# Column sums of six ctx blocks formed by accumulating transfers and two products, in a fused cross-attention and LoRA feed-forward kernel

## The chip, the cores and the metric

The kernel runs on one core of a Trainium2 chip. The metric is device time in microseconds (us) of one execution; several executions are taken and their median is given. The kernel before took 1082.93 us (median of three, 1082.42 to 1084.54). One further execution was recorded by the hardware profiler.

The core has five engines, each with an instruction queue that is worked off in order: PE (TensorE, matrix products, with its weight loads listed as PEld), DVE (VectorE), ACT (ScalarE), POOL (GpSimd) and SP (SyncE, used here to issue transfers). Sixteen DMA engines move data; transfers can be issued from the queues of SP, ACT and POOL. An engine that waits for another one's result, or for a transfer to land, waits at a semaphore, and everything behind that instruction in its queue waits too.

## What is computed

Two batches `b` of 1024 rows and 2048 columns go through two layers. The first is a product of two fake-quantised matrices, the second a linear layer with low-rank additions. Cut to what matters here:

```
q(v, s, z) = (clip(round(v / s + z), 0, 255) - z) * s
x = x + q(layernorm(x)) @ q(ctx)          # ctx: 2048 x 2048 for each b
x = x + ffn(layernorm(x))                 # kernel 2048 x 2048, bias, LoRA A and B by gate, shared LoRA
```

The kernel keeps the quantised values as whole numbers centred on 128, that is from -128 to 127, which 16-bit floats hold exactly. With c1 the centred x and c2 the centred ctx, and d1 = 128 - z1, d2 = 128 - z2, the product of one row and one column is

```
s1*s2 * ( sum_k c1*c2  +  d2 * rowsum(c1)  +  d1 * colsum(c2)  +  D*d1*d2 )
```

The column sums `colsum(c2)` are what the change is about: for each batch b and each block n of 512 columns of ctx, 512 sums over 2048 rows, wanted on all 128 partitions.

## The kernel before

**Tiling.** ctx comes in eight blocks (b, n), n = 0 to 3. A block of 2048 x 512 values is brought in as eight slices r of 128 partitions x 2 x 512 values (`lit` tiles, 512 KB each, loaded by SP). For every slice, ACT scales, rounds and clips below (`round_ctx`, L458, into one of three `q2b` tiles), and DVE clips above, subtracts 128 and writes bf16 into the block's two `big` tiles (`centre_ctx`, L464). A block's products with c1 (`Pair.products`, L530) go to PSUM for each of four groups g of 256 rows of x, each in two halves j. ACT or DVE add the column term and the row term to PSUM (`Pair.begin`, L526, before the products; `Pair.late`, L543, after them), and DVE scales and adds to `y` (`Pair.end`, L547).

**Column sums before the change.** `column_term` calls four steps. `column_parts` (L486) runs 16 products on PE, one for each 128 rows of the block, each with 32 columns of ones, so that four of them fill four strips of one PSUM tile `pcp`. `column_copy` (L499, DVE) brings the tile to SBUF. `column_mean` (L505, PE, float32, two passes) multiplies it with a matrix of 1/32, which adds the four strips and spreads the sum over all partitions (`pc`). `column_end` (L511, DVE) forms `d1 * colsum + D*d1*d2` in a `bp` tile, which `begin` and `late` read.

**Order.** For batch 0 the text STEPS sets the order of the entry: DVE, ACT and PE follow it step by step, each in its own part (`in_order`). In it V16 to V23 centre block (0,2), `u2 p2 c2 v2` are the four steps of its column term, `M2.0.0.6.7` and `M2.0.1.0.7` are products of that block, and `L2.0.0 L2.0.1` add its column term afterwards. Outside the entry a scheduler, with a cost model of its own, sets the order on each engine when the kernel is built. Block (0,3) is quantised during the products of block (0,2). Blocks (1,0) and (1,1) are quantised in the last outer step (o = 6) of the feed-forward of batch 0, from `meanwhile`; blocks (1,2) and (1,3) during the products of batch 1.

**Feed-forward.** Seven outer times seven inner products (Strassen's scheme, twice) in float32: `product` (L828), `spread` (L852), combinations of operands on POOL for the left side (`lit`, L762 and L771) and on DVE for the right side (`big`). `Delta.step` adds the low-rank part; its first two `bp` tiles of a batch come by a transfer that POOL issues (L679), the others by ACT.

Of the kernel before, what the change touches and what calls it, by code (L numbers as in the profile page):

```python
# [9 lines left out]

F32 = mybir.dt.float32
BF16 = mybir.dt.bfloat16
U8 = mybir.dt.uint8
I16 = mybir.dt.int16
AF = mybir.ActivationFunctionType
ALU = mybir.AluOpType
# [4 lines left out]
P = 128  # L21
# [4 lines left out]
QMAX = 255.0  # L26
CENTRE = 128.0
# [52 lines left out]
EARLY = [(0, 0), (1, 0), (2, 0)]  # L80
ROWS_ON_SCALAR = ()
PLACED_BY_SCALAR = (2, 3, 4, 5, 6, 7)


class Bufs:
# [13 lines left out]
def tile_quant_xattn_then_lora_ffn(  # L99
# [17 lines left out]
    nc = tc.nc  # L117
# [28 lines left out]
    lit = Bufs([const.tile([P, KQ, GT], F32, tag=f"lit{i}", name=f"lit{i}") for i in range(10)])  # L146
    q2b = Bufs([const.tile([P, 2, NB], I16, tag=f"q2b{i}", name=f"q2b{i}") for i in range(3)])

    acat = const.tile([P, KT, GPB // 2 * 3, R], F32, tag="acat", name="acat")
    own_col = [0, 2, 3, 5]  # L150

# [2 lines left out]
    axT = const.tile([P, GPB // 2, GT], F32, tag="axT", name="axT")  # L154
    gmat = const.tile([P, 2, GPB // 2, RC], F32, tag="gmat", name="gmat")
    st1 = const.tile([P, MT, NN, 6], F32, tag="st1", name="st1")
    st2 = const.tile([P, MT, NN, 6], F32, tag="st2", name="st2")
    r_s = const.tile([P, MT], F32, tag="r_s", name="r_s")

    zs = [  # L160
# [6 lines left out]

    def bf(t, n):

        return t.rearrange("p k n -> p (k n)").bitcast(BF16).rearrange("p (k n) -> p k n", n=n)  # L170

    def flat(t):
        return t.rearrange("p k n -> p (k n)")
# [91 lines left out]
    load_x(0, 3)  # L265
    ahead[0] = 10
    load_next()
    gate_b = const.tile([P, GB, NL], F32, tag="gate_b", name="gate_b")
    nc.sync.dma_start(
        out=gate_b.rearrange("p b n -> p (b n)"), in_=gate.rearrange("b n -> (b n)").partition_broadcast(P)  # L270
    )
# [23 lines left out]

    ident = const.tile([P, P], F32, tag="ident", name="ident")
    make_identity(nc, ident)
    ident_h = const.tile([P, P], BF16, tag="ident_h", name="ident_h")
    nc.gpsimd.tensor_copy(ident_h, ident)
    ones_h = const.tile([P, P], BF16, tag="ones_h", name="ones_h")  # L300
    nc.gpsimd.memset(ones_h, 1.0)


    zeros_h = const.tile([P, P], BF16, tag="zeros_h", name="zeros_h")
    nc.gpsimd.memset(zeros_h, 0.0)
    mean_w = const.tile([P, P], F32, tag="mean_w", name="mean_w")
    nc.gpsimd.memset(mean_w, 1.0 / 32)

# [8 lines left out]

    def gate_values():

        m_ad = const.tile([P, NL], F32, tag="m_ad", name="m_ad")  # L320
# [45 lines left out]
    class XTile:  # L366


        def __init__(self, b, m, c1T, wk):
            self.b, self.m, self.nm = b, m, f"{b}_{m}"  # L370
            self.on_vector = b == 0 and m not in ROWS_ON_SCALAR
            g, tok = m // MG, ds((m % MG) * P, P)
            self.y = y[g][:, m % MG, :]

            wf = flat(wk)
            self.q8 = wf[:, ds((m % 2) * (D // 4), D // 4)].bitcast(U8)
            self.qh = wf[:, D // 2 : D].bitcast(BF16)
            self.to = [c1T[g][:, ds(h * KH, KH), tok] for h in range(2)]
            self.pt = [None, None]

# [37 lines left out]
            )  # L418

        def turn(self, h):  # L420
            self.pt[h] = ps_m.tile([P, KH, P], BF16, tag="pm", name=f"pt_{self.nm}_{h}")
            for kt in range(KH):
                nc.tensor.transpose(self.pt[h][:, kt, :], self.qh[:, ds(h * H + kt * P, P)], ident_h)

# [23 lines left out]
            x.place(h)  # L448
        x.total()

    def quantise(c2, r):

        centre_ctx(c2, r, round_ctx())

    def round_ctx():
        buf, t = next_loaded(1)
# [3 lines left out]
        load_next()  # L460
        return qi

    def centre_ctx(c2, r, qi):
        nc.vector.tensor_scalar(c2[r // 4][:, ds(2 * (r % 4), 2), :], qi, QMAX, CENTRE, ALU.min, ALU.subtract)  # L464
        q2b.give(qi)

    def take_c2():
        bufs = [big.take() for _ in range(2)]
        return bufs, [bf(t, NB) for t in bufs]

    colt = {}
    pairs = []

    def column_term(b, n, c2):

        of = column_parts(b, n, c2)
        column_copy(of)
        column_mean(b, n, of)
        column_end(n, of)

    def column_parts(b, n, c2):

        parts = ps_m.tile([P, NB], F32, tag="pm", name=f"pcp_{b}_{n}")
        for k in range(KT):
            row = P // 4 * (k % 4)
            nc.tensor.matmul(  # L486
                parts[row : row + P // 4, :],
                ones_h[:, 0 : P // 4],
                c2[k // 8][:, k % 8, :],
                start=(k < 4),  # L490
                stop=(k >= KT - 4),
                skip_group_check=True,
            )
        return [parts]
# [18 lines left out]
    class Pair:  # L513
# [35 lines left out]
        def stats(self):  # L549
            for j in range(MG):  # L550
                nc.vector.bn_stats(  # L551
                    st2[:, self.g * MG + j, self.n, :], y[self.g][:, j, ds(self.n * NB, NB)]
                )

    def xattn_pair(b, n, g, c1T, c2):
# [66 lines left out]
    def prep_z(b, m, zq, wk):  # L622

        nm = f"{b}_{m}"
        g, tok = m // MG, ds((m % MG) * P, P)
        mean, rstd = norm_stats(st2[:, m], f"z{nm}")
# [295 lines left out]
    def entry():  # L922

        X = [XTile(0, m, c1T, wk) for m in range(MT)]
        qi, parts, at, ad = {}, {}, {}, {}
        idle = ps_acc.tile([P, MG, NB], F32, tag="delta", name="idle")
        recent = [(idle, 0)]
        tick = const.tile([P, 1], BF16, tag="tick", name="tick")

        def pair(n, g):  # L930
            if (n, g) not in at:
# [1 line left out]
            return at[n, g]  # L933

        def products(n, g, j, first, last=None):
            recent.append((pair(n, g).pa, j))
# [19 lines left out]
        def centred(r):  # L956
            if r // NR not in c2:
                next_block(0)
            centre_ctx(c2[r // NR], r % NR, qi.pop(r))

        def sums(n):
            parts[n] = column_parts(0, n, c2[n])

        def keep_busy(n):

            to, j = recent[-1]
            for i in range(n):
                nc.tensor.matmul(
                    to[:, j, :],
                    zeros_h,  # L970
                    (tick if to is idle else ones_h[:, 0:1]).to_broadcast([P, NB]),
                    start=(to is idle),
                    stop=True,
                    skip_group_check=True,
                )

        run = {
            "S": lambda m, n: X[m].stats(n),
# [9 lines left out]
            "Q": rounded,  # L988
            "V": centred,
            "u": sums,  # L990
            "p": lambda n: column_copy(parts[n]),
            "c": lambda n: column_mean(0, n, parts[n]),
            "v": lambda n: column_end(n, parts[n]),
            "B": lambda n, g, j: pair(n, g).begin(j),
            "M": products,
# [6 lines left out]
            "h": ad_copy,  # L1002
            "i": ad_turn,
            "j": lambda n: lora_a_place(n, ad[n]),
            "z": keep_busy,
# [14 lines left out]
    for b in range(B):  # L1020
# [9 lines left out]
        else:  # L1030
# [5 lines left out]
            for g in range(2, GPB):  # L1036
                for m in range(g * MG, (g + 1) * MG):
                    with tc.issue_after(opened.ins):
                        prep_x(b, m, c1T, wk)
                for n in range(2):  # L1040
                    xattn_pair(b, n, g, c1T, c2[n])
                    if g + 1 == GPB:
                        next_block(n)
                        if n == 0:
                            for r in range(NR):
                                quantise(c2[2], r)
# [9 lines left out]
        for g in range(GPB):  # L1056
            if (b, g) != (0, 0):
                xattn_pair(b, 2, g, c1T, c2[2])
            for r in {0: range(3), 1: range(3, 6), 2: range(6, 8), 3: ()}[g]:
                quantise(c2[3], r)  # L1060
            if 1 <= g <= 2:
                lora_a_step(b, g + 1)
            if g == 2:
# [53 lines left out]
        def meanwhile(o, s):  # L1117
# [23 lines left out]
                load_x(nb, m, slice(half * H, (half + 1) * H))  # L1141
            if s < 4:
                for r in range(2 * s, 2 * s + 2):
                    quantise(c2[0], r)
            if 1 <= s <= 4:
                prep_x(nb, s - 1, state["c1T"], state["wk"])
            if s == 3:
# [2 lines left out]
                c2[1] = [bf(c2b[1][0], NB)]  # L1150
            if s == 4:
                for r in range(2):
                    quantise(c2[1], r)
                c2b[1].append(big.take())
                c2[1].append(bf(c2b[1][1], NB))
            if s == 5:
                for r in range(2, 5):
                    quantise(c2[1], r)
            if s == len(INNER) - 1:
                for r in range(5, NR):  # L1160
                    quantise(c2[1], r)
# [62 lines left out]
```

## Time and profile before

| | |
|---|---|
| median of three executions | 1082.93 us (1082.42 to 1084.54) |
| the profiled execution | 1082.56 us |
| its span, from the first to the last instruction | 1080.8 us |
| PE busy | 1054.6 us (98%) |
| DVE busy | 766.6 us (71%) |
| ACT busy | 247.4 us (23%) |
| POOL busy | 253.8 us (23%) |
| transfers issued by POOL | 4 (`bp<-bd`, 256 KB each) |
| granted TensorE clock | 1.0 |

Numbers such as 84.80 are microseconds from the start of the span. A row of a group gives how often an instruction ran and its duration; for matrix products that duration includes their pipeline, so that the time between the starts of two of them, not the duration, is what one costs PE in a row. "To landing" is the time from the issue of a transfer to the semaphore that tells of its end.

### The profile page before, as it was taken

The page shows a single profiled execution, that of the slowest core. Times are in us where ns is not written, and L with a number is a line of the kernel's source. Part 1 is how long each engine was busy: PE and PEld are TensorE (multiplying, and loading weights), DVE is VectorE, ACT ScalarE, POOL GpSimd, SP SyncE. Part 2 cuts the span into 40 slices and gives each one's busy share as a digit, 9 for nine tenths or more (in the row PEclk, how much of TensorE's full clock was granted, in tenths as well). Part 3 has the DMA queues.
Part 4 walks back from the last instruction along what each step waited for, and adds up shares of the span by engine and source line. Part 5 has one row for each costly group of instructions (what it writes and reads, how often), then busy time and mean ns, then how long its engine had stood idle before and what let it go on. Part 6 is the DMA issues. An engine that isn't in the chain of part 4 may idle for free.

```text
span 1080.8 us, 10609 instructions
## 1 busy us (share of the span) xinstructions
PE 1054.6 (98%) x3932; PEld 489.8 (45%) x3932; DVE 766.6 (71%) x949; ACT 247.4 (23%) x351; POOL 253.8 (23%) x104
## 2 busy tenths in 40 slices
PE   5999999999999999999999999999999999999998
PEld 2443345544444444444444444554444444444443
DVE  7986867578877676677859655674969667756851
ACT  5866133210000000001675741331000000000000
POOL 0000003032435302533000000032244531253600
PEclk9999999999999999999999999999999999999999
DMA  9979645788798476699673292559889874748611
GB/s 341 381 196 308 190 176 190 256 316 295 263 339 324 160 264 217 191 372 321 230 246 119 98 266 103 198 210 360 294 269 297 288 269 148 264 146 301 214 39 58
DMA packets 119228, 257.15 MB, mean 238 GB/s; under 512 B 11272, under 2 KB 15496, under 8 KB 118152
## 3 DMA queue, kind: packets, MB, share of 16 engines
q1 hardware_dynamic: 98688, 215.05, 58.4%
q10 hardware_dynamic: 20168, 40.38, 10.7%
q0 software_dynamic: 320, 1.05, 0.4%
q8 instruction: 31, 0.51, 0.2%
q14 instruction: 21, 0.17, 0.1%
HBM read 220.79 MB, written 37.75 MB: 239 GB/s over the span
## 4 chain that ended last, share of the span: by engine, by line
PE 83%; DVE 8%; DMA 4%; ACT 3%; issue 1%; SPq 0%; ACTq 0%
PE fu L828 34%; PE fv L828 17%; PE pa L530 12%; PE fw L828 9%; PE pl L694 3%; PE px L648 3%; PE ptz L632 2%; DMA lit<-in_ctx_dram 2%; DVE st L551 2%; DVE st L383 1%; ACT q2b L458 1%; DVE y L547 1%; ACT big L412 1%; DVE big L771 1%; PE pg_b L574 1%
## 5 line engine op out<-in xcount | busy, mean ns | idle before, releaser
L828 PE MATMUL fu<-big,lit 128*128 128x512 f32 x896 | 395.3, 593 | 0.0
L828 PEld LDWEIGHTS fu<-big,lit 128*128 128x128 f32 x896 | 168.6, 190 | 206.3 <-issue 204.9
L530 PE MATMUL pa<-big,big 128*128 128x512 bf16 x1024 | 237.1, 381 | 7.3 <-ACT pa L526 3.4
L771 POOL TENSOR_TENSOR lit<-lit,lit 128x1024 f32<-128x1024 f32 x56 | 164.7, 2950 | 189.7 <-PE fw L828 74.6
L828 PE MATMUL fv<-big,lit 128*128 128x512 f32 x448 | 197.9, 594 | 0.0
L771 DVE TENSOR_TENSOR big<-big,big 128x2048 f32<-128x2048 f32 x56 | 164.4, 2935 | 0.7
L530 PEld LDWEIGHTS <-big 128*128 128x128 bf16 x1024 | 97.1, 98 | 136.3 <-issue 29.6
L762 POOL TENSOR_TENSOR lit<-lit,lit 128x1024 f32<-128x1024 f32 x32 | 85.7, 2677 | 256.4 <-DMA lit<-zs 230.4
L852 DVE TENSOR_TENSOR y<-y,fu 128x1024 f32<-128x1024 f32 x92 | 108.5, 1215 | 40.6 <-PE fu L828 40.2
L828 PEld LDWEIGHTS fv<-big,lit 128*128 128x128 f32 x448 | 84.3, 190 | 105.0 <-issue 104.7
L458 ACT ACTIVATE q2b<-lit,sc,inv 128x1024 int16<-128x1024 f32 x64 | 76.4, 1232 | 163.7 <-DMA lit<-in_ctx_dram 147.1
L852 DVE TENSOR_TENSOR y<-y,fv 128x1024 f32<-128x1024 f32 x48 | 56.8, 1218 | 78.8 <-PE fv L828 78.8
L762 DVE TENSOR_TENSOR big<-big,big 128x2048 f32<-128x2048 f32 x40 | 101.8, 2546 | 0.0
L828 PE MATMUL fw<-big,lit 128*128 128x512 f32 x224 | 99.4, 592 | 0.0
L683 ACT COPY pl<-bias 128x1024 f32<-128x1024 f32 x16 | 16.3, 1018 | 294.1 <-DVE y L705 258.1
L679 POOL DMA_DIRECT2D bp<-bd x4 | 2.6, 660 | 344.3 <-DMA bd<-q2b 166.3
L852 DVE TENSOR_TENSOR y<-y,fw 128x1024 f32<-128x1024 f32 x24 | 28.4, 1218 | 53.9 <-PE fw L828 53.9
L828 PEld LDWEIGHTS fw<-big,lit 128*128 128x128 f32 x224 | 42.1, 190 | 50.7 <-issue 50.7
L547 DVE SCALAR_TENSOR_TENSOR y<-pa,k_s,y 128x1024 f32<-128x1024 f32 x32 | 41.0, 1280 | 32.2 <-PE pa L530 32.1
L526 ACT ACTIVATE pa<-bp,r_s 128x512 f32<-128x512 f32 x58 | 39.0, 685 | 87.0 <-PE pa L530 57.1
L705 DVE TENSOR_TENSOR y<-pl,y 128x512 f32<-128x512 f32 x64 | 39.8, 679 | 17.5 <-PE pl L694 17.2
L383 DVE BATCH_NORM_STATS2 st<-y 128x6 f32<-128x512 f32 x64 | 41.4, 679 | 5.7 <-DMA y<-in_x_dram 5.6
(93 smaller groups left out, 629.6 us busy)
## 6 DMA issues: line engine op xcount, KB each, us to landing
big<-in_w_dram SPq DMA_DIRECT2D x96, 1024.0 KB
lit<-zs SPq DMA_DIRECT2D x80, 512.0 KB
lit<-in_ctx_dram SPq DMA_DIRECT2D x64, 512.0 KB
out_dram<-y ACTq DMA_DIRECT2D x30, 512.0 KB
zs<-lit ACTq DMA_DIRECT2D x24, 512.0 KB
lit<-in_lora_a_dram SPq DMA_DIRECT2D x32, 256.0 KB
lit<-in_lora_bt_dram SPq DMA_DIRECT2D x32, 256.0 KB
y<-in_x_dram SPq DMA_DIRECT2D x16, 512.0 KB
```

Of the source, the lines that this page charges most:

```text
L383: nc.vector.bn_stats(st1[:, self.m, n, :], self.y[:, ds(n * NB, NB)])
L458: nc.scalar.activation(qi, t, AF.Relu, bias=z2, scale=inv2)
L526: nc.scalar.activation(self.pa[:, j, :], colt[self.n], AF.Identity, bias=r_s[:, m : m + 1])
L530: nc.tensor.matmul(self.pa[:, j, :], self.c1T[:, k, ds(j * P, P)], self.c2[k // 8][:, k % 8, :], start=not self.begun[j], stop=(k == KT - ...
L547: return nc.vector.scalar_tensor_tensor(yp, self.pa, s12, yp, ALU.mult, ALU.add)
L648: nc.tensor.matmul(px[i * 2 * R : (i + 1) * 2 * R, :], acat[:, k, ds(3 * pr + i, 2), :].rearrange("p s r -> p (s r)"), zqs[i][k // KQ][:, ...
L694: nc.tensor.matmul(pl[j][i][:, half], axT[rows, pr, ds(j * P, P)], bt[rows, half], start=False, stop=True, skip_group_check=True,)
L705: line(nc.vector.tensor_add(yb, pl[j][i], yb))
L762: line(eng.tensor_tensor(got[0], got[0], got[1], ALU.add if terms[1][2] > 0 else ALU.subtract))
L771: line(eng.tensor_tensor(out_t, at[p], at[q], op))
L828: nc.tensor.matmul(ps[m], at[:, k, ds(m * P, P)], bt[:, k, :], start=(opens and k == 0), stop=(ends and k == KQ - 1), skip_group_check=True,)
L852: line(nc.vector.tensor_tensor(yp, yp, whole[chain], op))
```

## The change

For six of the eight blocks, (0,2), (0,3) and (1,0) to (1,3), the column sums are formed in another way. As soon as DVE has centred a slice (128 x 2 x 512), POOL issues a transfer of it into the SBUF tile `cs`: the first slice of a block as a copy, the other seven with an addition, so that `cs` ends as the sum of the eight slices. There is one `cs` tile for all blocks. PE then multiplies each of its two halves with a 128 x 128 matrix of ones, both into the same PSUM tile `pc`, and `column_end` reads that as before. `column_copy` and `column_mean` are not called for these blocks. Blocks (0,0) and (0,1) keep the old way.

All 16-bit tiles become float16 instead of bfloat16: c1, c2, the identity, the ones, `cs`. The sums of eight centred values are at most 1024 in size, which float16 holds exactly.

Room for `cs` is made in two ways: the statistics tile `st2` is dropped, with its users on `st1`; the gate's tiles `gate_b` and `m_ad` lie in `cs` until they have been used. Some unused helpers (`keep_busy`, `zeros_h`, `idle`) go.

```diff
-BF16 = mybir.dt.bfloat16
+F16 = mybir.dt.float16
...
+SUMMED_BY_DMA = ((0, 2), (0, 3), (1, 0), (1, 1), (1, 2), (1, 3))
...
+    cs = Bufs([const.tile([P, 2, NB], F16, tag=f"cs{i}", name=f"cs{i}") for i in range(1)])
...
-    st2 = const.tile([P, MT, NN, 6], F32, tag="st2", name="st2")
...
-    zeros_h = const.tile([P, P], BF16, tag="zeros_h", name="zeros_h")
-    nc.gpsimd.memset(zeros_h, 0.0)
...
-    def centre_ctx(c2, r, qi):
-        nc.vector.tensor_scalar(c2[r // 4][:, ds(2 * (r % 4), 2), :], qi, QMAX, CENTRE, ALU.min, ALU.subtract)
+    def centre_ctx(b, n, r, qi):
+        part = c2[n][r // 4][:, ds(2 * (r % 4), 2), :]
+        nc.vector.tensor_scalar(part, qi, QMAX, CENTRE, ALU.min, ALU.subtract)
         q2b.give(qi)
+        if (b, n) in SUMMED_BY_DMA:
+            if r == 0:
+                slices[n] = cs.take()
+                nc.gpsimd.dma_start(out=slices[n], in_=part)
+            else:
+                nc.gpsimd.dma_start(out=slices[n], in_=part, accum_op=ALU.add)
...
     def column_term(b, n, c2):
         of = column_parts(b, n, c2)
-        column_copy(of)
-        column_mean(b, n, of)
+        if (b, n) not in SUMMED_BY_DMA:
+            column_copy(of)
+            column_mean(b, n, of)
         column_end(n, of)

     def column_parts(b, n, c2):
+        if (b, n) in SUMMED_BY_DMA:
+            pc = ps_m.tile([P, NB], F32, tag="pm", name=f"pc_{b}_{n}")
+            for i in range(2):
+                nc.tensor.matmul(pc, ones_h, slices[n][:, i, :], start=(i == 0), stop=(i == 1))
+            cs.give(slices.pop(n))
+            return [pc]
...
-            "p": lambda n: column_copy(parts[n]),
-            "c": lambda n: column_mean(0, n, parts[n]),
+            "p": lambda n: (0, n) in SUMMED_BY_DMA or column_copy(parts[n]),
+            "c": lambda n: (0, n) in SUMMED_BY_DMA or column_mean(0, n, parts[n]),
```

More of the change, by code (lines that the diff above doesn't have):

```diff
@@ L168, in bf @@
     def bf(t, n):
-        return t.rearrange("p k n -> p (k n)").bitcast(BF16).rearrange("p (k n) -> p k n", n=n)
+        return t.rearrange("p k n -> p (k n)").bitcast(F16).rearrange("p (k n) -> p k n", n=n)
     def flat(t):
@@ L267, in tile_quant_xattn_then_lora_ffn @@
     load_next()
-    gate_b = const.tile([P, GB, NL], F32, tag="gate_b", name="gate_b")
+    gate_b = cs.spare[0].rearrange("p k n -> p (k n)").bitcast(F32)[:, 0 : GB * NL].rearrange("p (b n) -> p b n", n=NL)
     nc.sync.dma_start(
@@ L297, in tile_quant_xattn_then_lora_ffn @@
     make_identity(nc, ident)
-    ident_h = const.tile([P, P], BF16, tag="ident_h", name="ident_h")
+    ident_h = const.tile([P, P], F16, tag="ident_h", name="ident_h")
     nc.gpsimd.tensor_copy(ident_h, ident)
-    ones_h = const.tile([P, P], BF16, tag="ones_h", name="ones_h")
+    ones_h = const.tile([P, P], F16, tag="ones_h", name="ones_h")
     nc.gpsimd.memset(ones_h, 1.0)
-    zeros_h = const.tile([P, P], BF16, tag="zeros_h", name="zeros_h")
-    nc.gpsimd.memset(zeros_h, 0.0)
     mean_w = const.tile([P, P], F32, tag="mean_w", name="mean_w")
@@ L318, in gate_values @@
     def gate_values():
-        m_ad = const.tile([P, NL], F32, tag="m_ad", name="m_ad")
+        m_ad = cs.spare[0].rearrange("p k n -> p (k n)").bitcast(F32)[:, ds(GB * NL, NL)]
         nc.vector.tensor_reduce(m_ad, ident.rearrange("p (n r) -> p n r", r=RC), AX.X, ALU.add)
@@ L376, in __init__ @@
             self.q8 = wf[:, ds((m % 2) * (D // 4), D // 4)].bitcast(U8)
-            self.qh = wf[:, D // 2 : D].bitcast(BF16)
+            self.qh = wf[:, D // 2 : D].bitcast(F16)
             self.to = [c1T[g][:, ds(h * KH, KH), tok] for h in range(2)]
@@ L420, in turn @@
         def turn(self, h):
-            self.pt[h] = ps_m.tile([P, KH, P], BF16, tag="pm", name=f"pt_{self.nm}_{h}")
+            self.pt[h] = ps_m.tile([P, KH, P], F16, tag="pm", name=f"pt_{self.nm}_{h}")
             for kt in range(KH):
@@ L449, in prep_x, with quantise @@
         x.total()
-    def quantise(c2, r):
-        centre_ctx(c2, r, round_ctx())
+    def quantise(b, n, r):
+        centre_ctx(b, n, r, round_ctx())
     def round_ctx():
@@ L471, in tile_quant_xattn_then_lora_ffn @@
     colt = {}
+    slices = {}
     pairs = []
@@ L551, in stats @@
                 nc.vector.bn_stats(
-                    st2[:, self.g * MG + j, self.n, :], y[self.g][:, j, ds(self.n * NB, NB)]
+                    st1[:, self.g * MG + j, self.n, :], y[self.g][:, j, ds(self.n * NB, NB)]
                 )
@@ L625, in prep_z @@
         g, tok = m // MG, ds((m % MG) * P, P)
-        mean, rstd = norm_stats(st2[:, m], f"z{nm}")
+        mean, rstd = norm_stats(st1[:, m], f"z{nm}")
         for h, t in enumerate(halves(wk)):
@@ L925, in entry @@
         qi, parts, at, ad = {}, {}, {}, {}
-        idle = ps_acc.tile([P, MG, NB], F32, tag="delta", name="idle")
-        recent = [(idle, 0)]
-        tick = const.tile([P, 1], BF16, tag="tick", name="tick")
+        tick = const.tile([P, 1], F16, tag="tick", name="tick")
         def pair(n, g):
@@ L935, in products @@
         def products(n, g, j, first, last=None):
-            recent.append((pair(n, g).pa, j))
             for r in range(first, (first if last is None else last) + 1):
@@ L958, in centred @@
                 next_block(0)
-            centre_ctx(c2[r // NR], r % NR, qi.pop(r))
+            centre_ctx(0, r // NR, r % NR, qi.pop(r))
         def sums(n):
             parts[n] = column_parts(0, n, c2[n])
[L964 to L975, printed above, removed]
         run = {
@@ L1004, in entry @@
             "j": lambda n: lora_a_place(n, ad[n]),
-            "z": keep_busy,
         }
@@ L1045, in tile_quant_xattn_then_lora_ffn @@
                             for r in range(NR):
-                                quantise(c2[2], r)
+                                quantise(b, 2, r)
                                 if r % 4 == 3:
@@ L1059, in tile_quant_xattn_then_lora_ffn @@
             for r in {0: range(3), 1: range(3, 6), 2: range(6, 8), 3: ()}[g]:
-                quantise(c2[3], r)
+                quantise(b, 3, r)
             if 1 <= g <= 2:
@@ L1143, in meanwhile @@
                 for r in range(2 * s, 2 * s + 2):
-                    quantise(c2[0], r)
+                    quantise(nb, 0, r)
             if 1 <= s <= 4:
@@ L1152, in meanwhile @@
                 for r in range(2):
-                    quantise(c2[1], r)
+                    quantise(nb, 1, r)
                 c2b[1].append(big.take())
@@ L1157, in meanwhile @@
                 for r in range(2, 5):
-                    quantise(c2[1], r)
+                    quantise(nb, 1, r)
             if s == len(INNER) - 1:
                 for r in range(5, NR):
-                    quantise(c2[1], r)
+                    quantise(nb, 1, r)
                 column_term(nb, 1, c2[1])
```

## The prediction

> **What bounds the kernel now.** I read the page's busy times first, then the chain of waits, then the groups of the column sums, then the order of time around one of them.
>
> ```profile
> PE 1054.6 (98%) x3932; PEld 489.8 (45%) x3932; DVE 766.6 (71%) x949; ACT 247.4 (23%) x351; POOL 253.8 (23%) x104
> PE 83%; DVE 8%; DMA 4%; ACT 3%; issue 1%; SPq 0%; ACTq 0%
> ```
>
> PE is busy for 98% of the span and makes up 83% of the chain that ended last. So work taken from PE is time won, and a wait put into PE's queue is time lost, wherever it stands. What the column sums cost PE shows in the order of time around block (0,2):
>
> ```profile
> 92.19 0.43 DVE L464 TENSOR_SCALAR big<-q2b 128x1024 bf16<-128x1024 int16 x1 [0.70 <-ACT q2b L458]
> ...
> 94.88 1.05 PE L486 MATMUL pcp<-big,ones_h 128*32 128x512 bf16 x16
> 95.86 1.04 PE L530 MATMUL pa<-big,big 128*128 128x512 bf16 x4
> 96.82 1.10 PE L505 MATMUL pc<-q2b,mean_w 128*128 128x512 f32 x2
> 97.75 1.46 PE L530 MATMUL pa<-big,big 128*128 128x512 bf16 x6
> 97.96 0.81 DVE L511 TENSOR_SCALAR bp<-pc,k_s 128x512 f32<-128x512 f32 x1 [0.81 <-PE pc L505]
> ```
>
> The sixteen strip products hold PE from 94.88 to 95.86 us, 0.98 us (four strips run side by side), the spreading product from 96.82 to 97.75, 0.93 us. The last slice was centred at 92.62, only 2.3 us before PE needed the sum. That distance is what a transfer has to fit into. The transfers that POOL issues now are four, of 256 KB, the size of one slice:
>
> ```profile
> L679 POOL DMA_DIRECT2D bp<-bd x4: 538/624/852, 153.8 to 698.2; - x4
> ...
> DMA to landing us min/median/max: 3.9/5.6/7.1
> ```
>
> From issue to landing they took 6.9, 3.9, 7.1 and 4.2 us, taken one by one.
>
> **The change part by part.**
>
> *PE work removed and added.* Per block 0.98 + 0.93 = 1.91 us go. Two 128x512 products with 16-bit operands come; a product of line L530 costs 0.216 us in a row (34 in 7.5 us from 623.67), so 0.43 us, 0.5 with the change of weights. Net gain 1.4 us a block, 8.4 us for six. DVE loses six copies of 0.69 us, beside PE, worth nothing as such.
>
> *The chain of transfers.* In the built program each of POOL's transfers into `cs` waits for the centring of its slice and for the landing of the transfer before it, since all eight go to the same bytes. So a block's sum needs eight transfers end to end, and PE's first product with ones waits for the eighth. Centring comes every 1.1 us in (0,2), so the transfers set the pace. No row shows an adding transfer from SBUF to SBUF. The nearest are the four above, each from issue to landing. I take 3.9 us a transfer, the smaller value: 6.9 and 7.1 were each the first after a long rest of POOL, 3.9 and 4.2 the second. Upper end 5.6, the median. Lower end 2.5: in the trace's packet records the quickest began 1.4 us after issue, and its 64 packets of 4 KB at 0.16 us, four to an engine, are 0.64 us, with 0.4 us to the semaphore. An addition also reads its target, so I don't go lower for the range. Eight take 31.2 us (20 to 45).
>
> What covers that, block by block, from centring times and PE's place for the sum in the built program (in the time of before):
>
> (0,2): first slice centred at 85.2 (L464 at 84.80 plus 0.42), so the eighth lands at 116.4. PE arrives at 94.9; products of the same block stand behind the sum in the fixed order. Stall 21.5.
>
> (0,3): one `cs` tile, so its copy waits until PE has used the last sum. PE has 28.0 us of work from there to its next sum (95.86 to 125.73, less 0.93 for the spreading product and 0.9 for four products that now stand behind). Its slices are centred early. 31.2 - 28.0: stall 3.2.
>
> (1,0): first centring ends at 510.2, eighth landing 541.5 at best; PE arrives at 552.4. Hidden by float32 products of L828; no stall up to 5.2 us a transfer.
>
> (1,1): may start at 552.9, when PE has used the sum of (1,0); ends 584.1. The sum now stands 30 products later than the spreading product did (566.9), 573.4, less 2.4 us of removed work: 571.0. Stall 13.1.
>
> (1,2): first centring ends at 612.7, end 643.9. The sum stands 16 products later than before (620.9): 624.3. Stall 19.6.
>
> (1,3): waits for `cs` again; 96 products and two LoRA steps, 23.5 us, stand between the sums. Stall 7.7.
>
> Together 65.1 us. At 2.5 us a transfer the same working gives 10.3 + 0 + 0 + 1.9 + 8.4 + 0 = 20.6; at 5.6 it gives 35.1 + 16.8 + 2.6 + 26.7 + 33.3 + 21.3 = 135.8.
>
> The Trainium skill (DMA: Bandwidth & Descriptors, section "Two DMAs through the same engine are not ordered") speaks against the change: the issuer must wait for one transfer's semaphore before it issues another that depends on it. Its section "Anatomy of one DMA" prices one on this path at 2.0 us plus bytes/436e3, 2.6 us for a slice, where this trace has 3.9 to 7.1; as an estimate from that page the stalls would be 23 us.
>
> *Waits that become direct.* Behind the sum of (1,1) the next product needs the column term itself: L511 0.81, L526 0.67 and the hops between, 1.8 us, no longer covered; behind (1,2) four gate products cover 0.8 of it, 1.0 left. Together 2.8 us. Ends 0 and 10 (1.8 for each of the other four), where other products stand behind the sum.
>
> *PE's clock after a stall.* At the start of the kernel PE was slow after 8.0 us of idle time, and only near 20.5 us became fast:
>
> ```profile
> 13.14 1.03 PE L423 MATMUL pt<-ident_h,big 128*128 128x128 bf16 x8 [8.01 <-ACT big L412]
> 16.39 1.89 PE L530 MATMUL pa<-big,big 128*128 128x512 bf16 x4 [2.22 <-DVE big L428]
> ...
> 21.64 0.62 PE L423 MATMUL pt<-ident_h,big 128*128 128x128 bf16 x8
> ```
>
> Four products took 1.7 us of PE there against 0.86 later: 4.1 us at half speed, 2.05 us lost. It had not been fast before, so the row doesn't prove that a stall has this price; ends 0 and 2.05 for each of five stalls. I take it for the four stalls near or over 8 us: 8.2 us.
>
> *POOL and SP.* POOL's 48 issues at 0.54 to 0.85 us lie between 85 and about 650 us. One combination (L771 at 515.64) stands behind the second transfer of (1,0), which is issued at 514.1 when the first lands; if that takes 7.1 us the combination is 2.4 us late, and its user, the last inner product, starts over 20 us later. POOL's two `bp` transfers of each batch stand behind the chains of (0,3) and (1,3), done by the time PE has passed. Loads of w into freed `big` tiles and later centrings now also wait for transfers that read these tiles; PE itself has waited longer. All nothing; if the cover failed, it would be the same few us of one landing.
>
> *float16.* No row has it. Nearest are the 16-bit rows of L530 (0.216 us in a row); the far end is the float32 rows of L828 (0.43), with which 1024 products would cost 220 us more. Same width as bf16: I take 0. The shared statistics tile and `cs` for the gate are used by DVE at other times: 0.
>
> **Sum.** 65.1 - 8.4 + 2.8 + 8.2 = 67.7 us. The profiled execution took 1082.56 us, 1.8 of it outside the span and 0.4 under the median: 1150.3, said as 1150.
>
> **Rivals.**
>
> *A. The transfers fit (faster).* One mechanism: an adding transfer within SBUF, without HBM, takes less than about 1.6 us from issue to landing. Then (0,2) is ready at 98, (1,2) at 625.5, stalls sum to 4.3 us and no more, and the gain outweighs them: 1077 to 1082. For: slices come every 1.1 us and SBUF is near. Against: the least landing is 3.9 us, and the quickest had its first packet 1.4 us after issue.
>
> *B. Nearly hidden.* 1.7 to 2.5 us a transfer: 5 to 21 us of stalls, +1 to +18 us, 1084 to 1100. Against it the same rows.
>
> *C. Slower transfers.* 5.6 us or more, because the first chain starts while the DMA engines are 1.04 busy by the windows (85 to 95 us) and addition reads twice: 136 - 8.4 + 2.8 + 10.2 = +140, 1223. Against: loads stop when `lit` is full, so a long stall empties the engines.
>
> *D. The products lose more than they gain*, from float16 at another rate: up to 1300. Only the width speaks against it.
>
> **How the numbers follow.** The forecast (2.5 to 5.1 us a transfer) 0.80, A 0.05, B 0.07, C 0.06, D 0.02. The range is the forecast's: at 2.5 us 20.6 - 8.4 + 2.8 + 2 = +17, 1100; at 5.1 us 113 - 8.4 + 2.8 + 10 = +117, 1200. About 0.2% (2 us) is what a measurement can tell. Faster 0.05 (A), same 0.02 (the low end of B), slower 0.93.
>
> **What would show it.** In the profile after: group L494 (the products with ones) with idle time of PE before it ended by a transfer, some 20 us at (0,2) and (1,2), none at (1,0); transfers of POOL 3 to 5 us apart in a chain; landing of `cs` 3.9 us; the first products after a stall at 0.43 us apart; L544 (products, now f16) at 0.216 us. The prediction is wrong if the transfers of one block overlap, if they land in under 2 us, or if PE runs other products during the wait.

## The result: 11% slower, with six waits of PE at the sums

The changed kernel took 1202.53 us (median), the kernel before 1083.74 us beside it. The ratio is 1.1103, with a 95% interval of 1.1055 to 1.1151. The forecast was 1150 us with a range of 1100 to 1200: the direction was right, the loss 119 us instead of 68, and the time 2.5 us above the range.

The page of the changed kernel, in the lines that answer to those shown of before:

```profile
span 1200.5 us, 10553 instructions
PE 1058.1 (88%) x3836; PEld 490.5 (41%) x3836; DVE 762.2 (63%) x943; ACT 247.7 (21%) x351; POOL 288.1 (24%) x151
...
PE 73%; DMA 16%; DVE 5%; ACT 3%; issue 3%; SPq 0%; POOLq 0%; ACTq 0%; DVEq 0%
...
L494 PE MATMUL pc<-cs,ones_h 128*128 128x512 f16 x12 | 6.2, 621 | 117.4 <-DMA cs<-big 117.4
```

PE's busy time is about what it was (1054.6), but the span is 119.7 us longer. The last line says where: before the twelve products with ones PE stood idle for 117.4 us, and transfers into `cs` ended all of it. The same group asked for by its tile:

```profile
L471 POOL DMA_DIRECT2D cs<-big x42: 845/857/949, 91.8 to 765.0; - x42
L469 POOL DMA_DIRECT2D cs<-big x6: 562/570/697, 85.4 to 736.4; - x6
...
DMA to landing us min/median/max: 2.3/3.6/8.6
```

The median landing, 3.6 us, is close to the 3.9 us of the forecast. The maximum is not. The chain of waits of block (0,2) in order of time (start, duration, what) shows how the lengths lie:

```profile
91.76 8.44 DMA cs<-big
...
100.74 7.26 DMA cs<-big
...
108.54 4.49 DMA cs<-big
...
113.56 7.42 DMA cs<-big
...
121.51 3.28 DMA cs<-big
...
125.33 3.24 DMA cs<-big
...
129.10 3.26 DMA cs<-big
...
132.41 1.05 PE pc L494 x2
```

The links are strictly one behind the other, with 0.5 us between a landing and the next issue. The last three are 3.8 us apart from issue to issue, the earlier ones 5 to 9. The windows that lie between these issues (first the stretch and its length, then the busy time of PE, PEld, DVE, ACT and POOL, at the end the granted clock, the DMA engines' busy share and GB/s) show what differs; the first two lines are from block (1,0), the next three from (0,2), the last two from (1,2):

```profile
559.60:564.00 4.40, 4.40 (x11) 1.90 (x10) 4.40 (x6) 2.82 (x3) 3.27 (x2) 1.00 0.90 257
579.00:583.50 4.50, 4.50 (x25) 2.34 (x24) 3.27 (x7) 1.95 (x5) 0.85 (x1) 1.00 0.99 282
...
100.70:108.50 7.80, 0.00 (x0) 0.00 (x0) 0.85 (x2) 2.48 (x2) 0.87 (x1) 0.50 1.05 347
113.60:121.50 7.90, 0.00 (x0) 0.00 (x0) 0.00 (x0) 0.00 (x0) 0.82 (x1) 0.50 0.93 205
121.50:125.30 3.80, 0.00 (x0) 0.00 (x0) 0.00 (x0) 0.00 (x0) 0.86 (x1) 0.50 0.40 69
...
711.00:720.20 9.20, 0.00 (x0) 0.00 (x0) 0.00 (x0) 0.00 (x0) 0.85 (x1) 0.50 1.06 260
720.20:724.00 3.80, 0.00 (x0) 0.00 (x0) 0.00 (x0) 0.00 (x0) 0.85 (x1) 0.50 0.56 116
```

In the windows from 113.6 and 711.0 us, where a transfer took 7.9 and 9.2 us, DVE, ACT and PE did nothing at all, so none of them held POOL up; POOL's issue took 0.85 us as always. But the DMA engines were 0.93 and 1.06 busy, and SP's loads of lora_bt were running. From 121.5 us on, where the loads had stopped, the share was 0.4 and the transfer took 3.8 us; 69 GB/s in 3.8 us is 262 KB, this one transfer. The share alone does not give the length: the first two lines show 4.4 and 4.5 us at 0.90 and 0.99.

The packet records of the same trace say where the time goes. In a transfer without others beside it (121.5 us) the first packet begins 1.43 us after the issue, and its packets take 0.187 us each. In those issued at 91.8, 113.6 and 702.0 us the first packet begins 5.9, 5.6 and 5.7 us after the issue, and the packets take 0.18 us, no more. So most of the time added to these three is a late start, not slower packets. In the two transfers of 4.4 and 4.5 us the first packet came at 1.46 and 1.42 us.

With the mean length of a transfer that each chain had, the forecast's own working gives the stalls that were measured, to within 2 us. As the means come from the same trace, this tests its starts and covers, not the length:

| block | mean from issue to issue | stall by the forecast's working with it | measured stall | forecast at 3.9 us |
|---|---|---|---|---|
| (0,2) | 5.9 | 85.2 + 47.2 - 94.9 = 37.5 | 37.6 | 21.5 |
| (0,3) | 4.2 | 33.6 - 28.0 = 5.6 | 7.3 | 3.2 |
| (1,0) | 6.0 | 510.2 + 48.0 - 552.4 = 5.8 | 6.5 | 0 |
| (1,1) | 5.3 | 552.9 + 42.4 - 571.0 = 24.3 | 23.0 | 13.1 |
| (1,2) | 5.9 | 612.7 + 47.2 - 624.3 = 35.6 | 35.6 | 19.6 |
| (1,3) | 4.0 | 32.0 - 23.5 = 8.5 | 7.4 | 7.7 |

(The mean is the time from the first issue of a block to PE's first product with ones, over eight.)

### The profile page after: what moved, and what is told of

Same layout as the page of the kernel before. It is cut to its first block, busy times and chain, and to the rows that moved or that the text cites. A ratio compares the mean times of both kernels' runs of the same rounds, so it can differ in the third digit from the quotient of the medians.

```text
span 1200.5 us, 10553 instructions
## 1 busy us (share of the span) xinstructions
PE 1058.1 (88%) x3836; PEld 490.5 (41%) x3836; DVE 762.2 (63%) x943; ACT 247.7 (21%) x351; POOL 288.1 (24%) x151
## 4 chain that ended last, share of the span: by engine, by line
PE 73%; DMA 16%; DVE 5%; ACT 3%; issue 3%; SPq 0%; POOLq 0%; ACTq 0%; DVEq 0%
PE fu L842 31%; PE fv L842 16%; DMA cs<-big 13%; PE pa L544 10%; PE fw L842 8%; PE pl L708 3%; PE px L662 2%; PE ptz L646 2%; DMA lit<-in_ctx_dram 2%; DMA y<-in_x_dram 1%; ACT q2b L457 1%; ACT big L411 1%; PE pg_b L588 1%; DVE y L561 1%; DVE big L785 1%
## 5 line engine op out<-in xcount | busy, mean ns | idle before, releaser
L544 PE MATMUL pa<-big,big 128*128 128x512 f16 x1024 | 242.7, 389 | 6.8 <-ACT pa L540 3.1
L785 POOL TENSOR_TENSOR lit<-lit,lit 128x1024 f32<-128x1024 f32 x56 | 165.1, 2957 | 169.5 <-PE fu L842 45.0
L544 PEld LDWEIGHTS <-big 128*128 128x128 f16 x1024 | 99.7, 100 | 142.0 <-issue 37.3
L776 POOL TENSOR_TENSOR lit<-lit,lit 128x1024 f32<-128x1024 f32 x32 | 80.6, 2519 | 262.4 <-DMA lit<-zs 236.4
L494 PE MATMUL pc<-cs,ones_h 128*128 128x512 f16 x12 | 6.2, 621 | 117.4 <-DMA cs<-big 117.4
L471 POOL DMA_DIRECT2D cs<-big x42 | 36.3, 863 | 191.4 <-DMA cs<-big 142.4
L525 DVE TENSOR_SCALAR bp<-pc,k_s 128x512 f32<-128x512 f32 x8 | 6.5, 809 | 93.5 <-PE pc L494 93.0
```

Of the source, the lines that this page charges most:

```text
L471: nc.gpsimd.dma_start(out=slices[n], in_=part, accum_op=ALU.add)
L544: nc.tensor.matmul(self.pa[:, j, :], self.c1T[:, k, ds(j * P, P)], self.c2[k // 8][:, k % 8, :], start=not self.begun[j], stop=(k == KT - ...
L776: line(eng.tensor_tensor(got[0], got[0], got[1], ALU.add if terms[1][2] > 0 else ALU.subtract))
L785: line(eng.tensor_tensor(out_t, at[p], at[q], op))
```

## Experiments

The theory after the result: a transfer into `cs` takes 3.8 us alone and up to 9 us beside other transfers, eight of them are strictly in series, and PE waits for the rest. Rivals: the addition is slow in itself; something else in the change costs (float16, shared tiles, POOL); the traffic as such slows the rest of the kernel.

**Float16 and the shared tiles alone (e1_f16_only).**

```diff
-SUMMED_BY_DMA = ((0, 2), (0, 3), (1, 0), (1, 1), (1, 2), (1, 3))
+SUMMED_BY_DMA = ()
```

> The changed kernel with an empty list of blocks summed by transfers: float16, the shared statistics tile and the gate's place in cs stay, all column sums go the old way. If the whole loss is the wait for the transfers, the time is that of before, 1083 us, within 0.2%. If float16 or the shared tiles cost PE or DVE anything, it is above 1086; products of 128x512 would then show more than 0.216 us from start to start.

1083.02 us against 1083.17, ratio 0.9995 (0.9982 to 1.0009). Nothing else in the change costs or wins anything that this can measure; the whole loss belongs to the six blocks.

**The transfers, with nobody reading them (e2_unread).**

```diff
                 nc.gpsimd.dma_start(out=slices[n], in_=part, accum_op=ALU.add)
+                if r == NR - 1:
+                    cs.give(slices.pop(n))
...
-        if (b, n) in SUMMED_BY_DMA:
-            ...
-        if (b, n) not in SUMMED_BY_DMA:
-            column_copy(of)
-            column_mean(b, n, of)
+        column_copy(of)
+        column_mean(b, n, of)
```

The first removed lines stand in `column_parts`, the last ones in `column_term` and in the entry's p and c; every block's column means are formed as in the kernel before.

> All 48 transfers into cs are issued as in the changed kernel, but nothing reads cs: the column sums go the old way, by strip products, copy and float32 product. Theory (PE's wait is the whole loss): 1083 to 1088 us, and the lengths of the transfers, from issue to issue, still run from 3.8 us where other transfers are few to 7 to 9 us where the DMA engines are over 0.9 busy. Rival (13 MB more traffic and POOL's issues slow the loads or DVE): well above 1095 us, with PE waiting for lit or big loads.

1116.61 us, ratio 1.0308 (1.0285 to 1.0331): 33 us slower, though PE waits for no sum. This is a miss of the theory as stated, and the time is in the rival's window. The transfers themselves behaved as expected. In the chain of (1,2) POOL's issues (start, duration of the issue, in brackets what POOL waited for) were up to 10 us apart while PE was working:

```profile
639.57 0.89 POOL L471 DMA_DIRECT2D cs<-big  x1 [5.21 <-DVE acat L615]
648.12 1.11 POOL L471 DMA_DIRECT2D cs<-big  x1 [7.66 <-DMA cs<-big]
658.06 0.84 POOL L471 DMA_DIRECT2D cs<-big  x1 [8.83 <-DMA cs<-big]
666.35 0.85 POOL L471 DMA_DIRECT2D cs<-big  x1 [7.44 <-DMA cs<-big]
674.64 0.86 POOL L471 DMA_DIRECT2D cs<-big  x1 [7.44 <-DMA cs<-big]
678.46 0.86 POOL L471 DMA_DIRECT2D cs<-big  x1 [2.96 <-DVE bp L520]
```

Each issue comes 0.5 us after the landing of the transfer before, also where another engine is named. So the long transfers are not made by PE's stall. The span is 32.6 us longer than before: PE's idle time is 21.8 us more (48.0 against 26.2), and its busy time 10.8 us more, with the granted clock at 0.50 after several of these waits. One of the waits I traced: a chain which nobody waits for falls behind, and other work does wait for it. The two chains of batch 0 end near 196 us. POOL's first `bp` transfer, issued at 153.8 us in the kernel before, is issued at 193.5 here, with POOL's operand combinations behind it, and DVE waits for the transfers that still read a `big` tile before it may overwrite it:

```profile
196.39 2.98 DVE L780 TENSOR_TENSOR big<-big,big 128x2048 f32<-128x2048 f32 x1 [3.93 <-DMA cs<-big]
```

PE then stands 6.6 us before the transposes of the last group (201.1 us), the longest of these waits. The others, of 4.8 us and less, I did not trace: some can come from late loads, as the rival has it. In the changed kernel no such cost is to be seen: outside the six sums PE is idle for 25.0 us, before the change 26.2. That this is so because PE itself has already waited for each chain to end is my reading and not tested.

**Two chains side by side (e3_two_chains).**

```diff
             if r == 0:
-                slices[n] = cs.take()
-                nc.gpsimd.dma_start(out=slices[n], in_=part)
+                spare[n] = bias_b.take()
+                slices[n] = [cs.take(), spare[n].bitcast(F16).rearrange("p (k n) -> p k n", k=2)]
+            if r < 2:
+                nc.gpsimd.dma_start(out=slices[n][r], in_=part)
             else:
-                nc.gpsimd.dma_start(out=slices[n], in_=part, accum_op=ALU.add)
+                nc.gpsimd.dma_start(out=slices[n][r % 2], in_=part, accum_op=ALU.add)
```

> Two tiles take the slices in turn (even into cs, odd into the tile of the bias), PE adds them by four products with ones, so each chain is four transfers deep and two are in flight. Theory (a transfer's length is latency and turns behind other transfers, so two overlap): a block's sum is ready in 16 to 30 us, stalls of PE sum to 25 to 50 us, time 1110 to 1140. Rival (the sixteen engines' rate for additions is the limit): each transfer takes twice as long, stalls stay over 100 us, time near 1200.

1144.4 us (one execution), a little above the expected window. PE's stalls at the sums fall to 59.5 us together: 21.5 at (0,2), 14.9 and 3.6 for the two tiles of (1,1), 19.5 at (1,2); those of (0,3), (1,0) and (1,3) are gone. Two transfers in flight are each longer (median landing of all 48 transfers 6.6 us against 3.6), but the time of a block falls: from the first issue of (0,2) to PE's first product with ones it is 30.9 us in place of 47.0. So having eight in series rather than two chains of four is about half of the loss, and the rate at which the sixteen engines add is not the limit.

**Copies instead of additions (e4_copies).**

```diff
-                nc.gpsimd.dma_start(out=slices[n], in_=part, accum_op=ALU.add)
+                nc.gpsimd.dma_start(out=slices[n], in_=part)
```

> Every slice is copied into cs without addition, so cs ends as the last slice alone and the column sums are left out of what is computed; the chain of waits is unchanged. Theory (turns behind other transfers, one for every packet; a copy has 64 packets of 4 KB, an addition 128 of 2 KB): 2.9 us a transfer where the engines are quiet, 4 to 6 where they are busy, still about twice as long there; time 1125 to 1165. Rival 1 (the addition itself is slow): about 2.9 us everywhere, busy or not, time under 1115. Rival 2 (addition costs nothing, all is fixed latency): time stays near 1200.

1169.56 us (one execution), 4.6 above the expected window. In block (0,2) the first five copies took 34.3 us, the next ones 2.8 us each from issue to issue:

```profile
85.10:119.40 34.30, 9.42 (x46) 4.20 (x44) 9.21 (x21) 15.89 (x14) 2.83 (x5) 0.69 0.99 294
119.40:127.80 8.40, 0.52 (x2) 0.25 (x3) 0.00 (x0) 0.00 (x0) 1.61 (x3) 0.50 0.24 94
```

Alone, a copy is 1.0 us shorter than an addition (2.8 against 3.8). Beside the loads of this block it is hardly shorter: 6.9 us on average against 7.2 over the same five in the changed kernel (the first is a copy in both). So the addition is not what makes the transfers 5 to 9 us long. It is not free, either: with copies PE's stalls at the sums are 88.9 us in place of 117.4, and the time 33 us less. My picture of one turn for every packet, by which a copy with half the packets should have taken 4 to 6 us there, is not borne out. The packet records show a late start here too (first packet 3.1 to 4.5 us after the issue for the first three and the fifth copy, 1.1 us for the quiet ones). That other transfers make it long is argued from this and tested in the next experiment; what the first packet waits for is open.

**The lora_bt loads held back (e6_held_sum, e6_held_old).** DVE writes two elements of the column term of block (b,2) into each `lit` tile before the load into it; the second kernel does the same with no block summed by transfers.

```diff
+            if any(todo[0] is e for e in late) and not bt_open[0]:
+                return
...
+                if any(entry is e for e in late) and 2 in colt:
+                    nc.vector.tensor_copy(t[:, :, 0:1], colt[2][:, 0:2].unsqueeze(2))
                 for c, src in enumerate(srcs):
                     nc.sync.dma_start(out=t[:, c, :], in_=src)
```

> The changed kernel, with the loads of lora_bt (4 MB a batch) held back until the column term of block (b,2) is there: DVE writes two elements of that term into each lit tile before the load into it, so the loads cannot run beside the chain of (0,2) or (1,2). Theory (transfers into cs take turns with the loads at the DMA engines): in (0,2) the transfers issued after 100 us are 3.8 to 4.5 us apart (7.8, 5.0 and 7.9 in the changed kernel), the stall of PE falls from 37.6 to 24 to 30 us, that of (1,2) from 35.6 to 20 to 28; the loads then lengthen the chains of (0,3) and (1,3). Rival (POOL's issues are held up by the other engines, or the addition is slow by itself): both stalls stay within 3 us of what they were.

> The same held loads without any block summed by transfers, as the yardstick for the run before: 1083 to 1095 us, the difference to 1083 being what later lora_bt loads cost.

The yardstick took 1082.8 us: held loads cost nothing by themselves. With the sums it is 1202.46 us, no gain in total, but the chain of (0,2) changed where the loads were taken away. SP's last load before the sum was now issued near 104 us:

```profile
101.23 0.87 POOL L481 DMA_DIRECT2D cs<-big  x1 [7.61 <-DMA cs<-big]
108.71 0.85 POOL L481 DMA_DIRECT2D cs<-big  x1 [6.61 <-DMA cs<-big]
112.50 0.86 POOL L481 DMA_DIRECT2D cs<-big  x1 [2.93 <-DMA cs<-big]
116.33 0.86 POOL L481 DMA_DIRECT2D cs<-big  x1 [2.97 <-DMA cs<-big]
120.15 0.86 POOL L481 DMA_DIRECT2D cs<-big  x1 [2.96 <-DMA cs<-big]
123.92 0.86 POOL L481 DMA_DIRECT2D cs<-big  x1 [2.92 <-DMA cs<-big]
```

The transfer of 101.2 us still took 7.5 us, beside loads. From 108.7 us on all are 3.8 us apart, where the changed kernel had 5.0 and 7.9 among them. The stall went from 37.6 to 32.2 us and that of (1,2) from 35.6 to 29.6, both more than the rival's 3 us and less than I had expected; loads of ctx, lora_a and b_sh were still issued until 104 us. The loads then met the next chains: (0,3) went from 7.3 to 11.8 us, (1,3) from 7.4 to 11.0. Of the 11.4 us taken away at two sums, 8.1 came back at the two others, as the theory has it. The rest of the balance I did not trace; both kernels with held loads ran once.

**Block (1,0) alone (e5_only_10).**

```diff
-SUMMED_BY_DMA = ((0, 2), (0, 3), (1, 0), (1, 1), (1, 2), (1, 3))
+SUMMED_BY_DMA = ((1, 0),)
```

> Transfers for block (1,0) alone, which the forecast held to be covered. Theory (transfers take turns with loads): its chain runs while the DMA engines are 0.9 to 1.0 busy, the transfers take 5 to 7 us each, PE stalls 3 to 10 us before the sum, and the time is 1085 to 1095. Forecast as it stood (3.9 us a transfer): no stall, 1081 to 1083.

1092.51 us against 1082.69, ratio 1.0093 (1.0075 to 1.0112). The one block that I had held to be covered loses time as well: its transfers landed in 4.0 to 7.7 us, median 5.7, and PE waited 5.6 us. Other waits of PE make 1.9 us more (idle time 33.7 us against 26.2), and its busy time is 1.7 us longer in spite of the work removed: the granted clock was 0.50 for 3.4 us from 533.3 us, after a wait of 2.2, and again behind the sum.

**Other engines add, without transfers (e7_dve_adds, e9_dve_three, e10_dve_four, e8b_pool_some).** The same `cs` and the same two products with ones; the adding engine and the blocks vary.

```diff
             if r == 0:
                 slices[n] = cs.take()
-                nc.gpsimd.dma_start(out=slices[n], in_=part)
+                first_part[n] = part
             else:
-                nc.gpsimd.dma_start(out=slices[n], in_=part, accum_op=ALU.add)
+                nc.vector.tensor_tensor(slices[n], first_part.pop(n) if r == 1 else slices[n], part, ALU.add)
```

(In e8b_pool_some it is `nc.gpsimd`. The blocks: all six in e7; (0,2), (0,3), (1,0) in e9; these and (1,1) in e10; (0,3), (1,0), (1,1), (1,3) in e8b.)

> The same six blocks and the same two products with ones, but DVE adds each slice to cs right after centring it (seven additions of 128x1024 float16 a block), with no transfer. Theory (only the transfers' length lost the time; PE saves 1.4 us a block): if an addition takes under 0.8 us and hides beside PE, 1075 to 1081 us, with no stall of PE at the sums over 2 us. Rival (DVE, 71% busy, becomes late in the entry and in the quantising stretches): 42 additions of 0.6 to 1.1 us are 25 to 46 us of DVE, and the time is 1084 to 1100.

> DVE adds the slices for blocks (0,2), (0,3) and (1,0) alone; (1,1), (1,2) and (1,3) keep the strip products, because with all six PE waited 2.2 us behind the sum of (1,1) and 3.7 us near (1,2). Theory (PE saves 1.4 us a block where DVE has room): 1076 to 1080 us. Rival (the time won before batch 1's feed-forward is given back there, since its end is set by something else): 1081 to 1084.

> As with three blocks, and (1,1) as well. If the wait behind the sum of (1,1) is what cost the six-block kernel its gain, this is 1 to 3 us slower than with three blocks; if not, it is 1.4 us faster.

> GpSimd adds the slices itself, without transfers, for (0,3), (1,0), (1,1) and (1,3); the other four blocks keep the strip products. An addition of 128x1024 on GpSimd took 2.4 to 3.0 us in float32; seven are 17 to 21 us, in place of 34 to 48 us for eight transfers. Theory (only the length of the chain counts): sums are ready when PE comes, within 3 us, and the time is 1078 to 1085. Rival (GpSimd additions slow DVE down, or float16 additions take over 4 us): 1088 or more.

With all six on DVE: 1082.03 us, ratio 0.9994 (0.9983 to 1.0004), no difference, between the two windows expected. PE waits 0.8 us at one sum only, but 2.2 us behind the sum of (1,1) and 3.7 us near (1,2), where DVE and loads come late. With three blocks: 1075.09 us against 1082.54, ratio 0.9929 (0.9916 to 0.9943), faster than both kernels; with (1,1) as well 1076.92 us, 0.9946 (0.9933 to 0.9958). Adding on DVE for (1,1) thus costs 1.8 us where 1.4 was to be won, as the first of the two expectations had it; the other 5 us or so between three blocks and six belong to (1,2) and (1,3). The additions in the kernel with three blocks, and PE's totals:

```profile
L471 DVE TENSOR_TENSOR cs<-cs,big x18: 670/684/693, 87.7 to 528.2; 128x1024 f16<-128x1024 f16 x18
L495 PE MATMUL pc<-cs,ones_h x6: 379/379/390, 95.2 to 545.1; 128*128 128x512 f16 x6
...
PE 1049.5 (98%) x3884; PEld 488.8 (46%) x3884; DVE 770.9 (72%) x967; ACT 247.1 (23%) x351; POOL 251.2 (23%) x103
```

An addition on DVE takes 0.68 us, and PE waited for a sum only once, 0.8 us for that of (0,2). PE's busy time is 5.1 us less than before (1054.6), 1.7 us a block where the forecast had 1.4. The rest of the 7.5 us is in waits of PE that fell away (its idle time is 24.1 us against 26.2); which ones I did not trace.

On GpSimd (e8b_pool_some) an addition takes 2.13 us, without any landing to wait for. 1088.66 us, ratio 1.0056 (1.0043 to 1.007): slower than before, and in the rival's window. PE waits 3.9 us for the sum of (1,1) and 5.6 us at 529.6 us before transposes of x. The rival's reason is to be seen in front of the second wait: small DVE instructions, on which the transposes depend, took 1.4 and 1.7 us beside an addition of POOL. First the kernel with POOL's additions, then the same two instructions before:

```profile
526.59 4.42 POOL L471 TENSOR_TENSOR cs<-cs,big 128x1024 f16<-128x1024 f16 x2 [4.27 <-DVE nt_a L348]
527.39 1.43 DVE L395 SCALAR_TENSOR_TENSOR kx<-r_a,nt_a,inv 128x1 f32<-128x1 f32 x1
529.35 1.67 DVE L400 TENSOR_TENSOR ox<-mv_a,kx 128x1 f32<-128x1 f32 x1
...
526.12 0.20 DVE L396 SCALAR_TENSOR_TENSOR kx<-r_a,nt_a,inv 128x1 f32<-128x1 f32 x1
526.84 0.14 DVE L401 TENSOR_TENSOR ox<-mv_a,kx 128x1 f32<-128x1 f32 x1
```

That is 2.8 us of the 5.6; 1.1 us PE waited at this place before, too.

## Why the prediction was wrong where it was

- **What bounds the kernel, and PE's own saving.** Right. PE's wait is lost time wherever it stands, and e9_dve_three shows that the saving is there when the sum is ready in time (1.7 us a block).
- **The chain in series.** Right in form: eight landings, one `cs` tile, PE at the end. The table above shows that the places and the order of the stalls were right, and the covers to within 2 us.
- **The step that failed: "I take 3.9 us a transfer".** The term was mis-sized. Alone a transfer takes 3.8 us from issue to issue, so the value was a good one for quiet engines, in part by luck: an addition alone lands in 3.3 us, and the sum left out the 0.5 us from a landing to the next issue. But four of the six chains run beside SP's loads, with 4.4 to 9.2 us from issue to issue there and means of 5.3 to 6.0 us. I had read the windows (1.04 busy at 85 to 95 us), and put them under rival C with the remark that loads stop when `lit` is full. They do, near 121 us, after five of the eight transfers. And I explained 6.9 and 7.1 us in the trace of before by a rest of POOL; two of the rows (0.84 and 0.88 busy) also fit busy engines, but 4.2 us at 0.89 does not, so four rows could not settle it. The runs do: POOL had rested for 12.9 and 13.4 us before the transfers of 3.9 and 4.2 us, and for 9 us at most before the additions that took longer here. The lower end of 2.5 us also mixed two transfers: the one whose first packet came 1.4 us after its issue had packets of 0.31 us, not 0.16. The prediction took one length for all chains, and the lower one, where it should have taken a longer one for the stretches in which loads run; its range too ended at 5.1 us, under the means of these four chains. Its sum with the means of the table is 117 us of stalls in place of 65.
- **(1,0) "hidden up to 5.2 us a transfer".** The limit was right, the length was 6.0: 6.5 us of stall, and 9.8 us of loss when this block stands alone (5.6 of it at the sum).
- **PE's clock.** Taken at four times 2.05 us, found at more. The granted clock is 0.50 in those windows above in which PE stood, and the thirteen products after the sum of (0,2) took 4.95 us:

```profile
132.41 1.03 PE L494 MATMUL pc<-cs,ones_h 128*128 128x512 f16 x2 [37.62 <-DMA cs<-big]
133.23 4.95 PE L544 MATMUL pa<-big,big 128*128 128x512 f16 x13
```

  Twelve of PE's products, the two with ones among them, lay 0.40 to 0.43 us apart until 137.4 us, then 0.216. All six stalls had such a stretch, those of 6.5 to 7.4 us too. In these stretches PE was busy for 26.4 us at 0.50, so the clock cost about 13 us. PE's busy time agrees: it is 3.5 us more than before in spite of less work, 8.4 us by the forecast and 10 by the 1.7 us a block of e9_dve_three.
- **Waits that become direct.** 1.6 us behind (1,1), as forecast 1.8; none over 0.5 us behind (1,2), where 1.0 was forecast.
- **POOL, SP and float16 at nothing.** Right for the changed kernel (e1_f16_only, and outside the sums PE's idle time is no longer than before). The remark that PE itself waits longer may have carried more than I knew: without PE's wait the same transfers cost 33 us (e2_unread).
- **Rivals.** A and B fell: the shortest landing was 2.3 us, of a copy, and 3.2 to 3.3 of additions. C was right about the busy engines, less so about the second read (copies were as long beside the loads), and its price, 1223 us, went too far; the truth lay between it and the forecast. D fell with e1_f16_only. The estimate for such a transfer from the Trainium skill (DMA: Bandwidth & Descriptors, section "Anatomy of one DMA"), 2.6 us for a slice, is near what a copy took here with quiet engines (2.2 to 2.3 us to landing, 2.8 between issues), under the 3.2 to 3.3 us of an addition, and far from the 7 to 9 us of landings beside loads.

The 119.7 us by which the span grew are, in PE's time, 117.4 us of stalls at the sums, 2.4 of two other waits (0.8 at 616.9 us, 1.6 behind the sum of (1,1)) and 3.5 of longer busy time (the slower clock, less the work removed), less 3.6 of waits that PE had before and no longer has. This is an account and not a check: idle and busy time always add up to the span.

## What to carry to other kernels

A chain of accumulating transfers costs its number times the length from issue to issue (here the landing and 0.5 us), and that length has to be read for the stretch where the chain runs: look which loads run beside it before taking a duration from elsewhere in the trace. The DMA engines' share is a warning and no measure: at 0.90 to 1.08 the transfers here took 4.4 to 9.2 us. Off the critical path such a chain is not free either (e2_unread), since its tiles and the queue that issues it are held until it ends. If an engine with room can do the additions in 0.7 us each right after the values are made, as DVE does here for three blocks, the sum is ready when PE comes, within 0.8 us; where DVE has no room, as for all six blocks, nothing is won.

## What was unexpected of the hardware

- An accumulating transfer of 256 KB within SBUF took 3.8 us from issue to issue when it ran alone, and mostly 5 to 9 us beside loads; a plain copy 2.8 us alone, and 6.3 to 8.1 us beside the loads of block (0,2), where the two differ little. Most of the added time lies before the first packet: up to 5.9 us after the issue, 1.43 alone.
- POOL's issue of an addition takes 0.85 to 0.95 us, of a copy 0.56 to 0.70 us, busy engines or not.
- PE's granted clock fell to 0.50 at 3.7 to 4.9 us after it had stopped, and stayed there for 3.0 to 4.8 us after five of the six stalls, also after one of 6.5 us (4.1 us there); after (1,1), where a wait of 1.6 us follows, for 8.3 us. In e5_only_10 it was 0.50 for 3.4 us behind a wait of only 2.2 us.
- Beside POOL's additions of 2.13 us, DVE instructions of 0.14 and 0.20 us took 1.67 and 1.43 us (e8b_pool_some).
